# A graph attention layer on one core: the node stage moved beside the first chunk of edges

## The chip, the cores and the metric

The kernel runs on one core of one Trainium2 chip, in one launch. The core has TensorE (PE) for matmuls, VectorE (DVE), ScalarE (ACT), GpSimd (POOL) and SyncE (SP); SP, ACT and POOL also issue transfers, which share 16 DMA engines. Each engine takes its instructions in the order in which the compiled program lists them. The metric is the time on the device in microseconds (us), lower is better. Before the change the median of 18 runs is 6028.96 us (6012.63 to 6041.9).

## The reference

A layer norm with relu, one graph attention layer over 12500 nodes of 128 features and 412500 directed edges, and a residual. Cut to what is computed:

```python
h_in = jnp.maximum(_layernorm(x), 0.0)
h = h_in @ Wn + bn;  q = h_in @ Wq + bq;  k = h_in @ Wk + bk;  v = h_in @ Wv + bv
eh = edge_attr_64 @ We + be
attn_in = jnp.concatenate([q[src], k[dst], eh], axis=-1)
hmid = leaky_relu(attn_in @ A1 + b1, 0.2)
scores = leaky_relu(hmid @ A2 + b2, 0.2)
w = softmax(scores.mean(axis=-1), axis=0)          # over all edges
out = segment_sum(w[:, None] * v[dst], src, num_segments=12500)
y = h + out
return x + gamma * (y - y.mean(-1)) / sqrt(y.var(-1) + 1e-5) + beta
```

The edges are sorted by `dst`. The softmax runs over all edges at once, and the sum goes by `src`, which is in no order.

## The kernel before, in words

Nodes are padded to 12544, that is 98 blocks of 128, and edges to 403 groups of 1024 (eight tiles of 128). As the edges lie by `dst`, a group touches some 31 consecutive nodes. The groups are cut into four chunks of 86, 121, 121 and 75.

**Preparation.** `indices()` works out, on DVE, each edge's block and place by `src` and its offset in its group's window of 42 nodes (`WIN`) by `dst`; the window's first node stands in `base_i`. An edge outside its group's window would be left for `other_edges()`. The weights are folded (`w_all`, `w_ea`).

**Nodes.** `nodes()` handles 20 tiles of five blocks: load x (L552, SP), normalise (L361 to L372, DVE, with the square L365 and the root L370 on ACT), transposes (L561, PE), relu into `hT` (L563, ACT), one matmul with all weights (L569), and q, k, v each split into three bf16 parts by copies (L579, L587 on ACT, L581 on DVE) and matmuls that subtract what was copied (L582, L584). ACT then issues the writes of `hn_tab`, `q_tab` and `kv_tab` (L588 to L590). A tile holds, in each of the 128 partitions p, five neighbouring nodes of the 98 that begin at 98 p, so a transfer has one run of five rows per partition, and every window of `kv_tab` needs nodes of nearly all tiles.

**Finding slots.** `ready(c)` counts chunk c's edges by block (`count`, L391 to L408), plans (`plan`), and finds every edge a slot in the chunk's table (`place_slots`: per five edge tiles two matmuls L478, a reduction L522, a comparison L471, a small L526; every 40 edge tiles `settle`).

**First stage.** For each group `load` fetches edge features (L667), the window of k and v (L671) and the offsets (L673); `select` makes the selection matrix (L681, DVE). Per pair of edge tiles (four per group, called banks here) PE sums edge and node parts into `row_ps` (L705, L708). `evict` copies places into column 0 of four rows of a ring of 16 rows (L688, ACT, for every second bank) and the bank into two rows (L691, ACT), and POOL scatters each row tile into the chunk's table (L645, an indirect DMA): eight scatters per group. The ring holds two groups, so L688 of a group waits until the scatters of the group two before it have landed. The loads run two groups ahead, with three buffers.

**Second stage.** `second_stage()` reads the sorted table of the chunk before by blocks of 128 `src` nodes (L728) with the block's queries (L731), and works out scores, weights and sums.

**What sets the order.** The count, the plan and the first steps of slot finding, the 20 node tiles and the 98 clears of the first table's ends (`clear_ends`, L168, 257 KB each, SP) are interleaved first; there SP keeps the program's order and a scheduler, by its own costs, orders the other engines. `kv_tab` is read at addresses known only at run time, so a window waits for every `kv_tab` write that stands before it in the program. Then comes one pass per chunk: the first stage of chunk c, the second stage of chunk c-1, `ready(c+1)` and the clears of table c+1, interleaved; in these passes PE, DVE, ACT and SP keep the program's order (`manual_schedule`, L1026). The pass of the first chunk holds its first stage, the rest of its slots and `ready(1)`; the second stage begins after it.

Of the kernel before, what the change touches and what calls it, by code (L numbers as in the profile page):

```python
# [22 lines left out]
P = 128  # L23
# [30 lines left out]
NGRP = 5  # L54
CHUNKS = (0.213, 0.3, 0.3, 0.187)
# [3 lines left out]
def _ceil(a, b):  # L59
    return -(-a // b)  # L60
# [44 lines left out]
def kernel(ctx: ExitStack, tc: tile.TileContext, n_edges, x, src, dst, ea, w_nv, w_qt, w_kt,  # L105
# [43 lines left out]
    q_tab = dram.tile([NTN, P, 3 * D], BF, name="q_tab")  # L149
# [90 lines left out]

    early = ExitStack()
    weights = early.enter_context(tc.tile_pool(name="weights", bufs=1))
    w_all = weights.tile([P, 4, D], FP, name="w_all")
    bias_all = weights.tile([P, 4, D], FP, name="bias_all")
    early.enter_context(tc.manual_schedule(engines={ET.SP}))
# [6 lines left out]

    with tc.tile_pool(name="prep", bufs=1) as prep, tc.tile_pool(name="prep_ps", bufs=1, space=PSUM) as pps:
        nc.sync.dma_start(out=w_all[:, 0, :], in_=w_nv[0])
        nc.sync.dma_start(out=w_all[:, 3, :], in_=w_nv[1])
        a1_sb = prep.tile([P, 3, D], FP, name="a1_sb")
        nc.sync.dma_start(out=a1_sb, in_=a1.rearrange("(s p) d -> p s d", p=P))
        wt = prep.tile([P, 3, D], FP, name="wt")
        for i, w in enumerate((w_qt, w_kt, w_et)):
            nc.sync.dma_start(out=wt[:, i, :], in_=w)  # L260
        col = prep.tile([P, 3], FP, name="col")
        nc.sync.dma_start(out=col, in_=cols)
        fold = pps.tile([P, 4, D], FP, name="fold")
        for i in range(3):
            nc.tensor.matmul(fold[:, i, :], lhsT=wt[:, i, :], rhs=a1_sb[:, i, :], start=True, stop=True)
        nc.vector.tensor_copy(w_all[:, 1:3, :], fold[:, 0:2, :])
        for b in range(2):
            nc.vector.tensor_copy(w_ea[b * DE:(b + 1) * DE, b, :], fold[b * DE:(b + 1) * DE, 2, :])
        colb = prep.tile([P, 3, P], FP, name="colb")
        for i in range(3):  # L270
            nc.vector.tensor_copy(colb[:, i, :], col[:, i:i + 1].to_broadcast([P, P]))
        bias_ps = pps.tile([P, D], FP, name="bias_ps")
        for i in range(3):
            nc.tensor.matmul(bias_ps, lhsT=colb[:, i, :], rhs=a1_sb[:, i, :], start=(i == 0), stop=(i == 2))
        nc.vector.tensor_copy(bias_all[:, 0, :], row_bc[:, 0, :])
        nc.vector.tensor_add(bias_all[:, 1, :], bias_ps, row_bc[:, 2, :])
        nc.vector.memset(bias_all[:, 2, :], 0.0)
        nc.vector.tensor_copy(bias_all[:, 3, :], row_bc[:, 1, :])

# [11 lines left out]
    np_ = early.enter_context(tc.tile_pool(name="nodes", bufs=2))  # L291
    tps = early.enter_context(tc.tile_pool(name="t_ps", bufs=2, space=PSUM))
    mps = early.enter_context(tc.tile_pool(name="m_ps", bufs=4, space=PSUM))

    def indices():
# [14 lines left out]
        if t_end < NT:  # L310
# [7 lines left out]
        nc.vector.tensor_scalar(head, offset[0:1, :].rearrange("p (g k) -> p g k", k=SUPER)[:, :, 0],  # L318
                                float(NP - WIN), None, op0=ALU.min)
# [36 lines left out]
    indices()  # L356

    def normalise(pool, y, n):
# [12 lines left out]
        nc.vector.reciprocal(r[:, :n], r[:, :n])  # L371
        nc.vector.tensor_mul(y, y, r[:, :n].unsqueeze(2).to_broadcast([P, n, D]))  # L372

    x_v = x.rearrange("(p t) d -> p t d", p=P)
    hn_v = hn_tab.rearrange("(p t) d -> p t d", p=P)
    kv_v = kv_tab.rearrange("(p t) d -> p t d", p=P)
    q_v = q_tab.rearrange("t p d -> p t d")


    start_of = {}  # L380

    def count(c):

# [710 lines left out]
```

## Time and profile before

| | |
|---|---|
| median of 18 runs | 6028.96 us |
| the profiled execution | 6031.0 us, span 6029.3 us |
| first scatter | 372.75 us |
| first scatter of the second chunk (the 689th) | 1308.08 us |
| first load of a table block for the second stage (L728) | 1309.58 us |
| PE, DVE, ACT, POOL busy over the span | 83%, 74%, 35%, 56% |
| mean granted PE clock | 0.92 |

The span runs from the first to the last instruction of the profiled execution. Rows of a stage give the busy time of each engine between two moments, with the number of instructions, and then the PE clock that was granted (1 is full speed), the mean busy share of the 16 DMA engines and the GB/s that they moved. A row of waits names the engine and line that waited, what it waited for, the time in total, how often, and the longest. In the timeline a row has the start, the duration, the engine (with a q: the issue of a transfer), the line, the operation with the tile written and the tiles read, and in brackets the idle time before it and what ended it.

### The profile page before, as it was taken

The page shows a single profiled execution, that of the slowest core. Times are in us where ns is not written, and L with a number is a line of the kernel's source. Part 1 is how long each engine was busy: PE and PEld are TensorE (multiplying, and loading weights), DVE is VectorE, ACT ScalarE, POOL GpSimd, SP SyncE. Part 2 cuts the span into 40 slices and gives each one's busy share as a digit, 9 for nine tenths or more (in the row PEclk, how much of TensorE's full clock was granted, in tenths as well). Part 3 has the DMA queues.
Part 4 walks back from the last instruction along what each step waited for, and adds up shares of the span by engine and source line. Part 5 has one row for each costly group of instructions (what it writes and reads, how often), then busy time and mean ns, then how long its engine had stood idle before and what let it go on. Part 6 is the DMA issues. An engine that isn't in the chain of part 4 may idle for free. (4 is left out here: it accounts for less than half of the span.)

```text
span 6029.3 us, 99478 instructions
## 1 busy us (share of the span) xinstructions
PE 4997.8 (83%) x31822; PEld 3443.8 (57%) x32180; DVE 4461.5 (74%) x14096; ACT 2120.5 (35%) x5090; POOL 3391.9 (56%) x3236
## 2 busy tenths in 40 slices
PE   5766766669998899889999999989999999888880
PEld 3333433336666666556666666657777777666650
DVE  8765766658777777767777777767777777777779
ACT  2432222224333343334444434434444444333321
POOL 0047777777777777767777777756565555000000
PEclk8887678779999999989999999989999999999995
DMA  6755555568888888878898888877888887444433
GB/s 190 217 189 166 166 167 174 170 189 251 265 252 257 260 256 256 263 223 266 271 280 284 283 269 276 269 232 266 259 264 265 263 266 245 154 152 152 153 126 128
DMA packets 607563, 1362.14 MB, mean 226 GB/s; under 512 B 120100, under 2 KB 336860, under 8 KB 569016
## 3 DMA queue, kind: packets, MB, share of 16 engines
q1 hardware_dynamic: 423572, 880.87, 49.5%
q0 software_dynamic: 154704, 424.26, 19.5%
q10 hardware_dynamic: 28756, 50.57, 2.6%
q8 instruction: 255, 4.18, 0.3%
q14 instruction: 276, 2.26, 0.1%
HBM read 782.14 MB, written 573.14 MB: 225 GB/s over the span
## 5 line engine op out<-in xcount | busy, mean ns | idle before, releaser
L645 POOL DMA_INDIRECT tab<-row,slots x3223 | 3390.2, 1052 | 1726.6 <-issue 731.2
L705 PE MATMUL row_ps<-w_ea,ea_t 128*128 128x256 f32 x3224 | 1093.3, 424 | 292.4 <-ACT row L691 253.7
L691 ACT ACTIVATE row<-row_ps 128x512 f32<-128x512 f32 x1612 | 933.1, 588 | 477.5 <-PE row_ps L708 452.4
L859 PE MATMUL o_ps<-rows_of,w 128*128 128x128 f32 x7252 | 1081.8, 291 | 13.4 <-DVE w L850 12.4
L850 DVE TENSOR_SCALAR w<-iota_f,rows_of,score 128x128 f32<-128x128 f32 x3626 | 1021.8, 353 | 6.6
L776 DVE TENSOR_TENSOR rows_of<-h_ps,low 128x512 f32<-128x512 f32 (+1 forms) x980 | 634.8, 648 | 482.4 <-ACT low L775 480.6
L705 PEld LDWEIGHTS row_ps<-w_ea,ea_t 128*128 128x128 f32 x3224 | 601.2, 208 | 639.7 <-ACT row L691 424.5
L859 PEld LDWEIGHTS o_ps<-rows_of,w 128*128 128x128 f32 x7252 | 915.2, 195 | 43.9 <-DVE w L850 25.9
L775 ACT ACTIVATE low<-h_ps 128x512 f32<-128x512 f32 (+1 forms) x980 | 552.2, 563 | 870.5 <-PE h_ps L767 862.2
L767 PE MATMUL h_ps<-sel_q,qw 128*128 128x512 bf16 (+1 forms) x2582 | 720.7, 365 | 50.1 <-DVE sel_q L755 29.2
L708 PE MATMUL row_ps<-kv,sel 126*128 126x256 bf16 x3224 | 662.8, 289 | 12.0 <-DVE sel L681 12.0
L522 DVE TENSOR_REDUCE num<-run 128x5 f32<-128x500 f32 x646 | 433.4, 671 | 297.2 <-PE run L478 296.7
L764 PE MATMUL h_ps<-ident,rows_of 128*128 128x128 f32 x3626 | 572.9, 278 | 0.0
L784 PE MATMUL s_ps<-rows_of,a_sb 128*32 128x512 f32 (+1 forms) x1960 | 462.0, 586 | 65.1 <-DVE most_of L831 45.5
L688 ACT ACTIVATE row<-place 128x4 f32<-128x4 bf16 x806 | 162.9, 202 | 997.2 <-DMA tab<-row,slots 979.7
L801 PEld LDWEIGHTS s_ps<-heads,z 96*128 96x128 f32 (+1 forms) x3136 | 389.8, 193 | 206.6 <-DVE z L795 188.8
L708 PEld LDWEIGHTS <-sel 126*128 126x128 bf16 x3224 | 337.6, 105 | 291.0 <-issue 56.7
L764 PEld LDWEIGHTS h_ps<-ident,rows_of 128*128 128x128 f32 x3626 | 435.0, 143 | 109.1 <-issue 83.0
L801 PE MATMUL s_ps<-heads,z 96*128 96x3 f32 (+1 forms) x3136 | 412.6, 252 | 89.1 <-DVE z L795 88.7
L791 ACT ACTIVATE z<-s_ps,b_col 64x512 f32<-64x512 f32 (+1 forms) x392 | 266.9, 681 | 525.9 <-PE s_ps L784 525.3
L471 DVE TENSOR_TENSOR one<-bins_b,block 128x500 f16<-128x500 bf16 x646 | 431.3, 668 | 0.3 <-PE run L478 0.3
L755 DVE TENSOR_SCALAR sel_q<-pls,part 128x1408 bf16<-128x1408 uint8 (+2 forms) x392 | 331.6, 846 | 117.9 <-DMA pls<-pl_d 109.3
(178 smaller groups left out, 4808.5 us busy)
## 6 DMA issues: line engine op xcount, KB each, us to landing
rows_of<-tab SPq DMA_DIRECT2D x196, 1413.5 KB
ea_t<-in_ea SPq DMA_DIRECT2D x403, 256.0 KB
tab<-blank SPq DMA_DIRECT2D x392, 257.0 KB
rows_of<-tab SPq DMA_DIRECT2D x98, 1028.0 KB
rows_of<-tab SPq DMA_DIRECT2D x98, 899.5 KB
tab<-row,slots POOLq DMA_INDIRECT x3223
offs<-off_d SPq DMA_DIRECT2D x403, 126.0 KB
qw<-q_tab SPq DMA_DIRECT2D x392, 96.0 KB
```

The lines of the kernel that those rows point to most:

```text
L645: i = nc.gpsimd.indirect_dma_start(out=tabs[c][:, :], out_offset=bass.IndirectOffsetOnAxis(ap=slots[c][t // (8 * STR)][:m, t % (8 * STR):t ...
L691: nc.scalar.activation(row[:, :, 1:ROW], bank, AF.Copy)
L705: nc.tensor.matmul(bank[:, :, 0:D], lhsT=ea_g[:, ts(k, P)], rhs=w_ea, start=True, stop=False, skip_group_check=True)
L708: nc.tensor.matmul(bank[:, b, :], lhsT=sel[:, ts(b * halves + k, P)], rhs=kv, start=False, stop=True, skip_group_check=True)
L764: nc.tensor.matmul(h_ps[:, ts(j, P)], lhsT=rows_of[i][:, q * QUAD + j, 1:D + 1], rhs=ident, is_transpose=True, start=j == 0, stop=False, s ...
L767: nc.tensor.matmul(h_ps[:, 0:m * P], lhsT=qws[i][:, ts(k, D)], rhs=plss[i][:, q * QUAD * P:(q * QUAD + m) * P], start=False, stop=k == 2, ...
L775: nc.scalar.activation(low, h_ps, AF.Copy, scale=SLOPE)
L776: nc.vector.tensor_max(rows_of[i][:, q * QUAD:q * QUAD + m, 1:D + 1], h_ps.rearrange("p (j e) -> p j e", j=m), low.rearrange("p (j e) -> p ...
L784: nc.tensor.matmul(state["s_ps"][32 * q:32 * (q + 1), 0:m * P], lhsT=a2_sb, rhs=rows_of[i][:, q * QUAD:q * QUAD + m, 1:D + 1], start=True, ...
L801: nc.tensor.matmul(state["s_ps"][:, 0:nq * QUAD].rearrange("p (q j) -> p j q", j=QUAD)[:, j, :], lhsT=state["z"][:32 * nq, ts(j, P)], rhs= ...
L850: nc.vector.tensor_scalar(w, iota_f, rows_of[i][:, t, 0:1], state["score", i][:, t:t + 1], op0=ALU.is_equal, op1=ALU.mult)
L859: nc.tensor.matmul(state["o_ps"][:, 0:D], lhsT=w, rhs=rows_of[i][:, t, D + 1:ROW], start=t == 0, stop=t == ct - 1)
```

## The change

A node tile now holds 640 consecutive nodes (views `(t p) d` in place of `(p t) d`), so that the first windows need the first tiles alone. `q_tab` goes by node; the second stage reads a block's queries as rows that lie 98 nodes apart. Three node tiles are worked out ahead of the first chunk (`FIRST + 1`). The rest come inside its pass: before the window load of group g, `nodes_for(g)` puts as many tiles as are needed to have 1280 + 210 g nodes done (`FIRST`, `AHEAD`), one tile in about three groups, up to group 52. A window's base is held to what is done by then, `min(dst, NP - WIN, 1238 + 210 g)`. Writes of `kv_tab` are declared free of the windows read before. The node pools live until the end of the first chunk's pass, with one `t_ps` and three `m_ps` buffers instead of two and four, and the second stage's pools are opened after it. The first chunk's pass is no longer written out by hand on PE, DVE and ACT: only SP keeps the program's order, and the scheduler orders the others. The folding of the weights stands behind `indices()`.

```diff
@@ constants
+FIRST = 2
+AHEAD = 210
@@ tables
-    q_tab = dram.tile([NTN, P, 3 * D], BF, name="q_tab")
+    q_tab = dram.tile([NP, 3 * D], BF, name="q_tab")
@@ indices()
-        nc.vector.tensor_scalar(head, offset[0:1, :].rearrange("p (g k) -> p g k", k=SUPER)[:, :, 0],
-                                float(NP - WIN), None, op0=ALU.min)
+        bound_i = xp.tile([1, NG], I32, name="bound_i")
+        nc.gpsimd.iota(bound_i, pattern=[[AHEAD, NG]], base=FIRST * NGRP * P - WIN, channel_multiplier=0)
+        bound = xp.tile([1, NG], FP, name="bound")
+        nc.vector.tensor_scalar(bound, bound_i, float(NP - WIN), None, op0=ALU.min)
+        nc.vector.tensor_tensor(head, offset[0:1, :].rearrange("p (g k) -> p g k", k=SUPER)[:, :, 0], bound, op=ALU.min)
@@ views
-    hn_v = hn_tab.rearrange("(p t) d -> p t d", p=P)
-    kv_v = kv_tab.rearrange("(p t) d -> p t d", p=P)
-    q_v = q_tab.rearrange("t p d -> p t d")
+    x_c, hn_c, kv_c, q_c = (v.rearrange("(t p) d -> p t d", p=P) for v in (x, hn_tab, kv_tab, q_tab))
+    win_loads = []
@@ nodes()
-            nc.sync.dma_start(out=xt[:, :n, :], in_=x_v[:, t0:t0 + n, :])
+            nc.sync.dma_start(out=xt[:, :n, :], in_=x_c[:, t0:t0 + n, :])
...
-            nc.scalar.dma_start(out=hn_v[:, t0:t0 + n, :], in_=hn[:, :n, :])
-            nc.scalar.dma_start(out=q_v[:, t0:t0 + n, :], in_=parts[:, :n].rearrange("p t s d -> p t (s d)"))
-            nc.scalar.dma_start(out=kv_v[:, t0:t0 + n, :], in_=parts2[:, :n].rearrange("p t s d -> p t (s d)"))
+            i = nc.scalar.dma_start(out=kv_c[:, t0:t0 + n, :], in_=parts2[:, :n].rearrange("p t s d -> p t (s d)"))
+            for other in win_loads:
+                tc.declare_no_dep(i.ins, other, reason="windows before lie in nodes that were done by then")
+            nc.scalar.dma_start(out=hn_c[:, t0:t0 + n, :], in_=hn[:, :n, :])
+            nc.scalar.dma_start(out=q_c[:, t0:t0 + n, :], in_=parts[:, :n].rearrange("p t s d -> p t (s d)"))
@@ before the chunks
-    first_ready = ready(0)
-    interleave((some_steps(first_ready, ready_enough()), ready_enough()), (nodes(), _ceil(NTN, NGRP)),
-               (clear_ends(0), NTN))
+    np_ = setup.enter_context(tc.tile_pool(name="nodes", bufs=2))
+    tps = setup.enter_context(tc.tile_pool(name="t_ps", bufs=1, space=PSUM))
+    mps = setup.enter_context(tc.tile_pool(name="m_ps", bufs=3, space=PSUM))
+    node_loads = nodes()
+    done = [0]
+
+    def nodes_for(g):
+        while done[0] * NGRP * P < min(NP, FIRST * NGRP * P + AHEAD * g):
+            next(node_loads)
+            done[0] += 1
+
+    first_ready = ready(0)
+    def first_nodes():
+        for i in range(FIRST + 1):
+            nodes_for(_ceil(i * NGRP * P - FIRST * NGRP * P + 1, AHEAD))
+            yield
+
+    interleave((some_steps(first_ready, ready_enough()), ready_enough()), (first_nodes(), FIRST + 1),
+               (clear_ends(0), NTN))
@@ first_stage(), load(g)
-            nc.sync.dma_start(out=kv, in_=win_v[ds(state["bases"][i % 8] * 3, 3 * WIN), :])
+            nodes_for(g)
+            i = nc.sync.dma_start(out=kv, in_=win_v[ds(state["bases"][i % 8] * 3, 3 * WIN), :])
+            win_loads.append(i.ins)
@@ second_stage(), load(i)
-            nc.sync.dma_start(out=qws[i], in_=q_tab[b])
+            nc.sync.dma_start(out=qws[i], in_=q_tab.rearrange("(p t) d -> t p d", p=P)[b])
@@ the passes
-        with tc.manual_schedule(engines={ET.PE, ET.DVE, ET.Activation, ET.SP}):
+        if c == 0:
             interleave(*jobs)
+            for _ in node_loads:
+                pass
+            setup.close()
...
+        else:
+            with tc.manual_schedule(engines={ET.PE, ET.DVE, ET.Activation, ET.SP}):
+                interleave(*jobs)
```

What order the compiled programs have on ACT in the first chunk can be read without running them. Here p9a and p9b are the copies of places (L688) for the first and second two banks of group 9, r9 the four evictions (L691) of group 9, sq and sqrt L365 and L370, hT L563, KV the issue of a tile's `kv_tab` write (L590), and the node tile's other copies stand between hT and KV:

```
before  ... p7a r7(0,1) p7b r7(2,3) p8a r8(0,1) p8b r8(2,3) p9a r9(0,1) p9b r9(2,3) ...
after   ... KV r7(0-3) p9a r8(0,1) p9b r8(2,3) r9(0,1) p10a r9(2,3) p10b sq p11a sqrt p11b hT hT KV r10(0-3) ...
```

## Prediction

> **What bounds the kernel now.** I read the busy table and the 40 slices first, then the busy time by stage, then who waited for whom inside the first chunk, then the timeline where the node stage ends.
>
> ```profile
> span 6029.3 us, 99478 instructions
> POOL 0047777777777777767777777756565555000000
> 0.00:373.00 373.00, 231.13 (x1458) 125.12 (x1459) 273.93 (x875) 146.04 (x475) 1.95 (x14) 0.84 0.70 203
> 373.00:1309.00 936.00, 613.11 (x3091) 343.78 (x3090) 604.41 (x1685) 212.90 (x523) 711.03 (x689) 0.78 0.52 168
> 1309.00:6030.00 4721.00, 4153.56 (x27274) 2974.93 (x27632) 3583.11 (x11538) 1761.60 (x4092) 2678.89 (x2535) 0.95 0.76 239
> ```
>
> The stage rows give busy us of PE, PE's weight loads, DVE, ACT and POOL, then the granted clock, the DMA share and GB/s. POOL, which issues the row scatters, does nothing for 373 us while the nodes are worked out. Then the first chunk's 688 scatters run from 372.75 to 1308.08, 1.36 us each, with POOL busy 76% and PE and DVE at 65%: this stage is set by the rate of scatters, and everything after it moves with its end.
>
> ```profile
> ACT row L688 <- DMA tab<-row,slots: 577.8, 145, 8.8
> POOL tab L645 <- DMA kv<-kv_tab: 370.4, 1, 370.4
> POOL tab L645 <- issue: 163.9, 538, 0.3
> 342.91 0.59 ACT L563 ACTIVATE hT<-tp 128x512 f32<-128x512 f32 x1
> 349.63 0.34 ACTq L590 DMA_DIRECT2D kv_tab<-parts  x1
> 361.39 0.34 ACTq L590 DMA_DIRECT2D kv_tab<-parts  x1
> 366.41 0.41 SPq L671 DMA_DIRECT2D kv<-kv_tab  x1
> 370.41 0.75 DVE L681 TENSOR_SCALAR sel<-offs,third 126x1024 bf16<-126x1024 uint8 x1 [9.84 <-DMA offs<-off_d]
> 371.86 0.60 ACT L691 ACTIVATE row<-row_ps 128x512 f32<-128x512 f32 x1 [10.33 <-PE row_ps L708]
> 372.75 1.36 POOL L645 DMA_INDIRECT tab<-row,slots  x1 [370.38 <-DMA kv<-kv_tab]
> ```
>
> Two things are to be seen. First, within the first chunk ACT stands still for 577.8 us of 936 at L688, the copy of the places into the row ring, because the scatters that read the ring (16 rows, two groups) have not landed. Today that is harmless: nothing else is queued on ACT in this stage. Matching L688 with the scatter it waits for, the wait ends 3.4 us (median; 2.6 to 5.4 from the tenth to the ninetieth of 144 waits) after that scatter's start. Second, from a node tile's last table write to the first scatter that depends on it take 372.75 - 361.39 = 11.4 us: write 5.0, window and offsets 4.0, selection, matmul and eviction 2.3.
>
> **The change part by part.**
>
> *Start of the scatters.* Only three of the 20 node tiles stand ahead of the first window. DVE is busy 273.9 us before the first scatter; a node tile costs it 9.7 us (its rows L361 to L372, L573, L574, L581 sum to 194 us for 20), so 17 tiles take 165 away and leave 109, which at today's 73% share is 149 us. The third tile's x load stands on SP behind 82 clears of 257 KB, 21.6 MB; with the indices and two tiles some 31 MB, that is 107 us at 290 GB/s (203 divided by its share 0.70) or 152 at 203, from 15 us on: at 122 to 167, say 145. Behind it come its load and normalisation (about 13), its matmuls (11, below) and the 11.4 above. First scatter at 180, with overheads 185 (165 to 215): 188 us earlier (158 to 208).
>
> *Node tiles inside the first chunk.* The other 17 tiles come one per three groups, before the loads of groups 4, 7, ... 52. Their engine time fits: per three groups at today's pace (33 us) DVE has some 31 us of work and PE about as much, if everything overlapped. It does not, because of the order in which the compiled program puts ACT's instructions. From the cycle of groups 7 to 9 (row = L691, place = L688): rows of 7, 8 and 9, place 10, sq, place 11 first half, sqrt, place 11 second half, hT (L563), the tile's copies, the kv_tab write (L590), rows of 10. Place 11 second half overwrites ring rows that group 9's last four scatters read. So hT waits on ACT until every scatter issued so far has landed; and group 10's window, one of this tile's nodes, can only be loaded after its kv_tab write. The same stands in all 17 cycles. POOL runs dry once per tile. What is queued behind the waiting place copy is ACT's whole node tile, behind that DVE's and PE's parts of it, SP's window load (with the clears and loads of later groups behind it), and at last POOL.
>
> One such drain: landing 3.4 (2.6 to 5.4), place copy 0.2, hT to the kv_tab write 11 (6.7 in the lines above, where a tile had ACT nearly to itself; 11.2, 12.5 and 14.3 at 265.80, 280.35 and 295.29, with counting work between; the changed order puts about four steps of slot finding between, so I take the lower of these), write to first scatter 11.4 (10 to 14: the write is 960 KB against 576, but the queue ahead is emptier), less the 1.36 of an ordinary step. 24.6 us (18 to 32), times 17: 418 (306 to 544).
>
> The other waits sit under this. The x load waits on SP for the ea buffer of the group three earlier, free some 8 us into the next cycle; load and normalisation then have the 31 us of 24 scatters. DVE's steps of slot finding (0.68 + 0.67 + 0.17 us, and 2.1 us from one to the next at 371 to 379) stall with the node tile, but about ten of 15 per cycle fit in the drain. If that cover were too small, each further step would add 2.1 us a cycle.
>
> *Order of the rest of the chunk.* From group 65 on the place copies of the next two groups stand ahead of the next group's rows, so ACT waits for a landing every second group: 11 times (3.4 + 0.2 + 0.6 + 0.3 - 1.36 = 3.1), 34 us (0, if POOL is late anyway, to 60).
>
> *Edits at nothing.* The x, hn and kv_tab transfers go from 2560 and 7680 bytes a run to 512 and 1536, the bytes are the same and the first chunk uses 0.52 of the DMA engines; if that failed, the write's 5.0 us grow, which the 14 above holds. The queries of the second stage are still 768 bytes a run, loaded many steps ahead; today 392 loads of 96 KB (0 to +20 us if their spread rows are slower). The window bound (1238 + 210 per group) lies above the data's 31 nodes per group, so no edge is left over. Weights and prep move behind the indices: a few us, in the 185. Later chunks keep their order.
>
> The Trainium skill (DMA: Bandwidth & Descriptors, Anatomy of one DMA) puts a transfer's fixed cost at about 2.0 us. By that a drain would lose 1.4 on the landing, about 0.8 on the 960 KB write (2.0 plus 2.2 at its 436 GB/s) and 1.8 on the window and offsets, and the 17 would cost 350, the sum 6227; the trace's 3.4, 5.0 and 4.0 decide.
>
> *Sum,* against the profiled execution's 6031.0 us (its span is 6029.3; the median of 18 runs is 6029.0, so 2 less): -188 + 418 + 34 = +264, 6295; on the median 6293, and I say 6290.
>
> **The rivals.**
>
> Faster, by hidden nodes: ACT finds the ring's scatters landed when it reaches the place copies, so hT runs beside the scatters. For it: at today's start of the chunk (L688 in the first four groups) there is no wait, and PE and DVE have a third of their time free. Against: 145 of the later copies waited, and in the new order ACT evicts three groups in a burst, well ahead of POOL. Price: 6031 - 188 = 5843 in full; it decides once a drain costs under (188 - 34) / 17 = 9.1 us, less than the 11.4 of the table path alone.
>
> Half drains: hT waits only for the group before the last, so some ten of the 25 us lie under the last eight scatters (8 times 1.36 = 11). 17 times 14 = 238, sum +84: 6115. For it: some tiles have their first hT ahead of the last place copy (three of 17). Against: their copies stand behind it all the same.
>
> Longer drains: DVE's slot finding, held up behind the waiting node tile, is not caught up, five steps of 2.1 us more a cycle: 17 times 35 = 595, sum +441, 6470. For it: DVE's order is fixed too, and PE's granted clock, 0.78 now, may fall when PE idles (0.59 in the last 180 us, where PE is busy 16%). Against: ten steps fit in the drain.
>
> Not what it says: the first scatter comes hardly earlier, at 300, since SP's clears hold the third x load. Then +264 + 115 = 6410. Against: 290 GB/s is enough for them.
>
> **How the numbers follow.** Full drains 68%, half drains 12%, longer drains or a late start 12%, hidden nodes 6%, no change to be measured 2%. The likeliest alone: 6160 (start 208 earlier, drains 19 us each, tail 15) to 6420 (start 170 earlier, drains 31, tail 30). The range takes in half drains and most of the longer: 6095 to 6440. About 0.2% is what can be told from no change: faster 6%, same 2%, slower 92%.
>
> **What would show it.** After: first scatter near 185 us; POOL in the first chunk with 17 gaps of some 25 us, each ended by an eviction that waited for PE, PE for the selection, that for the offsets; ACT's place copies ahead of each hT waiting for the scatters; the first load of rows_of near 1570; later stages as long as before. I am wrong if POOL's gaps are under 10 us, if they end at the x load or at DVE's slot finding, or if the stages after the first chunk change by more than 20 us.

## The result, and the profile after

The changed kernel takes 6384.25 us (median of 8 runs, 6370.55 to 6391.17) against 6031.07 for the kernel before beside it: a ratio of 1.0585, with a 95% interval of 1.0574 to 1.0596. It is slower, by 353 us. The profiled execution took 6372.4 us.

From its page, the span and POOL's busy tenths over the 40 slices:

```profile
span 6370.7 us, 99183 instructions
...
POOL 0334433476577777776777777775555555100000
```

And the busy time by stage (us, then PE, weight loads, DVE, ACT and POOL busy, the granted clock, the share of the DMA engines, GB/s): before the first scatter, the stretch with node tiles, the rest of the first chunk, everything after it.

```profile
0.00:225.00 225.00, 89.31 (x893) 48.99 (x894) 147.60 (x464) 26.57 (x80) 2.12 (x14) 0.74 0.86 178
225.00:1239.00 1014.00, 567.30 (x2755) 293.68 (x2756) 514.57 (x1518) 256.50 (x712) 418.56 (x417) 0.70 0.40 128
1239.00:1648.00 409.00, 227.68 (x772) 118.93 (x772) 199.99 (x503) 87.30 (x203) 275.80 (x273) 0.72 0.50 157
1648.00:6371.00 4723.00, 4154.86 (x27404) 2969.93 (x27761) 3603.03 (x11615) 1762.50 (x4097) 2672.86 (x2535) 0.95 0.76 239
```

The last row says where the time is not: everything from the second chunk on takes 4723 us, before 4721. The first scatter comes at 225.07 instead of 372.75 (147.7 earlier), the 689th at 1647.78 instead of 1308.08. The first chunk went from 935 to 1423 us, and in its first 1014 us no engine is busy for more than 56%: DVE 51%, PE 56%, POOL 41%. It waits. In that stretch POOL has 17 gaps, one per node tile, from 19.7 to 34.2 us, 488 in all, 28.7 on the mean. (A gap is counted here from the start of one scatter to the start of the next; the idle time in brackets is some 1 us shorter.) One of them in the timeline, all engines in order of time:

```profile
354.61 0.46 SPq L527 DMA_DIRECT2D xt<-in_x  x1
...
382.27 0.96 POOL L662 DMA_INDIRECT tab<-row,slots  x1 [0.31 <-issue]
384.94 0.21 ACT L707 ACTIVATE row<-place 128x4 f32<-128x4 bf16 x1 [4.65 <-DMA tab<-row,slots]
385.05 0.58 ACT L538 ACTIVATE hT<-tp 128x512 f32<-128x512 f32 x1
402.05 0.38 ACTq L563 DMA_DIRECT2D kv_tab<-parts  x1
406.36 0.36 SPq L689 DMA_DIRECT2D kv<-kv_tab  x1
412.51 1.09 ACT L710 ACTIVATE row<-row_ps 128x512 f32<-128x512 f32 x2 [10.31 <-PE row_ps L727]
413.38 0.96 POOL L662 DMA_INDIRECT tab<-row,slots  x1 [30.15 <-ACT row L710]
```

This is the chain of the prediction, link by link: the last scatter (382.27), the place copy that waits for its landing (384.94), hT directly behind it, the tile's work on ACT up to the table write (402.05), the window load that waits for that write (406.36), the eviction, the next scatter. Over the 17 gaps the medians are 2.8 us from the last scatter to hT, 15.9 from hT to the write, 10.7 from the write to the scatter. Who waited for whom in the first chunk (us in total, times, longest) shows ACT's wait for landings much as before (577.8 us then), and POOL's wait for an eviction, 20.5 us before:

```profile
ACT row L707 <- DMA tab<-row,slots: 606.6, 165, 10.5
POOL tab L662 <- ACT row L710: 525.6, 82, 33.2
```

So the chain stood as foretold, in 12 of the 17 cycles with a place copy directly ahead of hT; in the other five the tile's root stands there and hT follows its transposes. Whether each link *causes* the loss is another question, and there the experiments did not follow the prediction.

### The profile page after: what moved, and what is told of

Its sections match the earlier page's. It is cut to its first block, busy times and chain, and to the rows that moved or that the text cites. A ratio compares the mean times of both kernels' runs of the same rounds, so it can differ in the third digit from the quotient of the medians.

```text
span 6370.7 us, 99183 instructions
## 1 busy us (share of the span) xinstructions
PE 5039.1 (79%) x31822; PEld 3431.5 (54%) x32180; DVE 4465.2 (70%) x14097; ACT 2132.9 (33%) x5090; POOL 3369.3 (53%) x3237
## 5 line engine op out<-in xcount | busy, mean ns | idle before, releaser
L878 PEld LDWEIGHTS o_ps<-rows_of,w 128*128 128x128 f32 x7252 | 909.7, 194 | 45.7 <-DVE w L869 27.8
L700 DVE TENSOR_SCALAR sel<-offs,third 126x1024 bf16<-126x1024 uint8 x403 | 305.1, 757 | 194.1 <-DMA offs<-off_d 188.3
```

What stands on the lines that cost most here:

```text
L878: nc.tensor.matmul(state["o_ps"][:, 0:D], lhsT=w, rhs=rows_of[i][:, t, D + 1:ROW], start=t == 0, stop=t == ct - 1)
```

## Experiments

They ran on three chips, which differ in the later stages (see the last section), so each ratio is to the kernel before on the same chip, and the first chunk is read by itself. "Chunk" is the time from the first scatter to the 689th; "gaps" is the mean of the 17 longest gaps in it, without the one at the chunk's border. They lie at the 17 node tiles, but for the two kernels with freed windows, where some of the tiles' gaps are too short to count among them.

| kernel | chip | ratio to before (95%) | first scatter | chunk | gaps |
|---|---|---|---|---|---|
| changed | (first comparison) | 1.0585 (1.0574 to 1.0596) | 225 | 1423 | 28.7 |
| changed, once more | C | 1.0566 (1.0538 to 1.0594) | 231 | 1518 | 31.6 |
| program order | A | 1.0428 (1.0387 to 1.0470) | 225 | 1461 | 28.3 |
| program order, ACT and SP only | A | 1.0534 (1.0502 to 1.0566) | 224 | 1555 | 34.1 |
| tile three groups ahead | A | 1.0448 (1.0429 to 1.0466) | 227 | 1458 | 28.7 |
| all nodes first | A | 1.0179 (1.0162 to 1.0195) | 396 | 1126 | none |
| tile ahead, windows freed | B | 1.0239 (1.0213 to 1.0265) | 219 | 1222 | 12.9 |
| ring of 32 rows | B | 1.0621 (1.0590 to 1.0651) | 252 | 1425 | 29.1 |
| first tiles early | B | 1.0616 (1.0588 to 1.0645) | 241 | 1440 | 29.4 |
| fine tiles | B | 0.9877 (0.9846 to 0.9907) | 264 | 971 | none |
| no place copies | C | 1.0512 (1.0490 to 1.0535) | 229 | 1492 | 31.4 |
| no place copies, tile ahead, windows freed | C | 1.0131 (1.0107 to 1.0154) | 218 | 1247 | 13.0 |
| fine tiles, lead grows | C | 0.9924 (0.9905 to 0.9943) | 245 | 1100 | none |

The kernel before takes 6600 us on chip A, 6068 on B, 6611 on C. The changed kernel itself, run again on chip C:

> The changed kernel as it is, beside the three kernels below on one chip, since the chips differ in the stages after the first chunk (4723 to 5232 us). Expected: 1.056 to 1.063 times the kernel before, 17 gaps with a mean of 28 to 31 us, first scatter at 220 to 255.

Its ratio is the same within the intervals; its gaps, 31.6 us, lie just above the 28 to 31 expected.

### The order on ACT

The theory on record was that the scheduler's place copies, put ahead of hT, make ACT wait for all scatters. The first test gives the first chunk back its written order.

```diff
-            interleave(*jobs)
+            with tc.manual_schedule(engines={ET.PE, ET.DVE, ET.Activation, ET.SP}):
+                interleave(*jobs)
```

> The changed kernel with one edit: the first chunk's PE, DVE, ACT and SP instructions run in the order in which the program emits them, as the later chunks' do. On ACT a node tile's squares, root, hT, copies and kv_tab write then stand together, behind the rows of the group just before and ahead of the next group's place copies. Theory (the scheduler's place copies, put ahead of hT, make ACT wait for all scatters, so POOL is drained once per tile): hT no longer waits for a landing; the tile's 17 us on ACT and the 11 us from its write to the next scatter run beside the last group's 8 to 16 scatters (11 to 22 us). The 17 gaps of POOL shrink from 28.7 us to 8 to 16, so 220 to 350 us less than the changed kernel's 6384: 6035 to 6165. Rival (the cause is not the order on ACT but the chain tile, write, window, whichever way it is ordered): the gaps stay at 25 us or more and the time at 6340 or more.

> As the program-order kernel, but only ACT's and SP's instructions of the first chunk keep the program's order; PE and DVE stay with the scheduler. Theory (ACT's order alone is what drains POOL): the same as with all four engines, 6035 to 6165 us, gaps of 8 to 16 us. Rival (DVE's slot finding or PE's order holds the node tile): gaps stay near 28 us and the time near 6384, and only the kernel with all four engines in program order is faster.

The gaps did not shrink: 28.3 and 34.1 us. (By their ratios, times 6031, the two would take 6289 and 6353: both outside the theory's range, and the first below its rival's 6340 as well.) One gap of the kernel with all four engines in program order, all engines in order of time:

```profile
417.25 0.43 SPq L527 DMA_DIRECT2D xt<-in_x  x1
419.78 0.96 POOL L662 DMA_INDIRECT tab<-row,slots  x1 [0.30 <-issue]
...
427.36 0.60 ACT L538 ACTIVATE hT<-tp 128x512 f32<-128x512 f32 x1 [2.29 <-PE tp L536]
...
445.54 0.39 ACTq L563 DMA_DIRECT2D kv_tab<-parts  x1
...
448.05 1.06 ACT L710 ACTIVATE row<-row_ps 128x512 f32<-128x512 f32 x2
448.90 0.96 POOL L662 DMA_INDIRECT tab<-row,slots  x1 [28.16 <-ACT row L710]
```

No landing is waited for ahead of hT, and no window behind the write (write to scatter 3.4 us instead of 10.7; the windows of these rows had been loaded). In their place the tile comes in one piece: x is loaded only 2.5 us before the last scatter, hT starts 7.6 after it, the tile takes 18.2 us on ACT (20.6 in the median of 17), and the rows of the next group stand behind it on PE, DVE and ACT alike. With ACT's order alone the square waits up to 29.3 us for DVE. The theory's sentence "the tile's 17 us run beside the last scatters" was wrong: POOL had at most a few scatters left when the tile began. The lower ratio with all four engines (1.0428; the changed kernel has 1.0566 on chip C and was not run on chip A) is not found in the 17 gaps; one part is the chunk's border, 2.3 us instead of 19.3, and the rest was not traced.

### The windows

> The changed kernel with one edit: each load step takes the group's window first and then the node tile that the group three later needs, so no window waits for a tile that was only just written; the scheduler still orders the first chunk. Theory (two parts in a row make a drain: landing, place copy and 17 us of ACT's tile ahead of the next rows, and 11 us from the tile's write to the next scatter): only the second part goes, since ACT still waits for the landings ahead of hT. The gaps go from 28.7 to 18 to 22 us, 17 times 7 to 11 us less: 6200 to 6265. Rival 1 (the window chain alone is the cause): no gaps above 5 us, 5900 to 5960. Rival 2 (it hides nothing, since the ring's waits set all): 6384 within 30.

```diff
             kv = p2.tile([3 * WIN, 2 * D], BF, name="kv")
-            nodes_for(g)
             i = nc.sync.dma_start(out=kv, in_=win_v[ds(state["bases"][i % 8] * 3, 3 * WIN), :])
             win_loads.append(i.ins)
+            nodes_for(g + 3)
```

The gaps are 28.7 us, the changed kernel's own: none of the theory's 7 to 11 us a gap is to be seen. (By its ratio it would take 6301, which is in neither the theory's range nor the rival's; the changed kernel was not run on this chip, and the gaps don't hold the difference.) By the gaps the second rival comes nearest, but not for its reason. A window waits for every write of `kv_tab` that stands before it in the program, whether it reads from it or not. With the tile put earlier, the tile just written is a later one, and the window waits for it all the same. One gap:

```profile
365.30 0.96 POOL L662 DMA_INDIRECT tab<-row,slots  x1 [0.30 <-issue]
...
382.18 0.38 ACTq L563 DMA_DIRECT2D kv_tab<-parts  x1
386.45 0.40 SPq L688 DMA_DIRECT2D kv<-kv_tab  x1
...
392.78 0.96 POOL L662 DMA_INDIRECT tab<-row,slots  x1 [26.52 <-ACT row L710]
```

So the next kernel also says which writes a window does not need (`start` is a tile's first node):

```diff
+            node_writes.append((t0 * P, i.ins))
...
             win_loads.append(i.ins)
+            for start, other in node_writes:
+                if start >= FIRST * NGRP * P + AHEAD * g:
+                    tc.declare_no_dep(i.ins, other, reason="the window lies in nodes before this tile")
```

> As the kernel with tiles three groups ahead of their windows, with one more edit: a window's load no longer counts as depending on the kv_tab writes of tiles that it doesn't need (there every window waited for every table write emitted before it, so SP and POOL still stood until the tile just written was in the table). The rows of the next group can now run beside the tile. Theory (the drain is held by the windows' wait for the newest tile; once that is gone only the place copies that stand ahead of hT and of the kv_tab write wait for landings): the 17 gaps of 28.7 us fall to one or two waits of 4 to 10 us per tile, 10 to 18 us a tile, 180 to 320 us off the changed kernel; on a chip where that takes 6384, 6065 to 6205. Rival (the place copies ahead of hT alone drain POOL, the windows don't matter): gaps stay at 20 us or more, less than 150 us off.

This took the gaps to 12.9 us and the chunk to 1222 us. Two kernels on the same chip whose windows still wait as in the changed one, with the ring of 32 rows and with the early first tiles, have 29.1 and 29.4 us and chunks of 1425 and 1440. The changed kernel's ratio would give 6423 on this chip, so it is some 215 us faster, inside the range. One gap:

```profile
429.62 0.58 ACT L539 ACTIVATE hT<-tp 128x512 f32<-128x512 f32 x1
...
447.12 0.96 POOL L664 DMA_INDIRECT tab<-row,slots  x1 [0.30 <-issue]
450.97 0.38 ACTq L564 DMA_DIRECT2D kv_tab<-parts  x1
455.23 0.40 SPq L690 DMA_DIRECT2D kv<-kv_tab  x1
...
462.60 0.96 POOL L664 DMA_INDIRECT tab<-row,slots  x1 [14.52 <-ACT row L715]
```

hT now runs 24.8 us (median) before the last scatter ahead of the group that needs the tile: rows are made beside the tile. What is left is the table path, write to window to eviction, 13.3 us in the median. It is left because the tile is worked on for three groups, so its write comes (median) 1.9 us before that last scatter, when the window that needs it is next. The place copies still wait here (512.8 us in total from 220 to 1300), so the part that the prediction named first is there, and the gaps are short all the same.

"Needs" is by the bound of 1280 + 210 g nodes, which the edit above uses, and not by the data. At some 31 nodes a group the windows of all 86 groups of the first chunk end near node 2670, in the fifth tile, so only two of the 17 tiles inside the chunk are ever read by them; the others are wanted by the later chunks and by the second stage. A tighter bound for the windows alone, at the same pace of the tiles, would free nearly all of them; no run tried it.

### The landing ahead of hT

> The changed kernel with one edit: the first chunk's row ring has 32 rows instead of 16 (four groups), so the place copies ahead of hT wait for scatters that were issued two groups earlier; the windows' wait for the newest tile stays. Theory 1 (ACT's wait for the landing of the last scatters ahead of hT starts the drain): hT runs beside the last 8 to 16 scatters, so 10 to 20 us of the tile's 17 and the table path's 11 are hidden; the gaps fall from 28.7 to 9 to 18 us, 180 to 330 us off the changed kernel (6055 to 6205 where that takes 6384). Theory 2 (the tile's x load, behind the ea buffers on SP, or its chain through DVE sets when hT runs): gaps within 3 us of 28.7, less than 60 us off.

```diff
+    rring0 = setup.enter_context(tc.tile_pool(name="pr0", bufs=1)).tile([P, 2 * RROWS, ROW], FP, name="row")
...
-            at = ((g - g0) * halves + k) * 2 % RROWS
-            row = rring[:, at:at + 2, :]
+            ring, depth = (rring0, 2 * RROWS) if c == 0 else (rring, RROWS)
+            at = ((g - g0) * halves + k) * 2 % depth
+            row = ring[:, at:at + 2, :]
```

The gaps are 29.1 us, which looks like theory 2, but the test did not take away what it meant to:

```profile
411.00 0.96 POOL L663 DMA_INDIRECT tab<-row,slots  x1 [0.30 <-issue]
413.77 0.21 ACT L709 ACTIVATE row<-place 128x4 f32<-128x4 bf16 x1 [4.76 <-DMA tab<-row,slots]
413.88 0.58 ACT L538 ACTIVATE hT<-tp 128x512 f32<-128x512 f32 x1
```

The copy ahead of hT still waits for the last scatter (2.77 us after its start). In the compiled order the scheduler had used the deeper ring to put the place copies two groups further ahead, to the rows of the group just before. So this run does not decide between the two. The next one leaves the copies out:

```diff
+    nc.gpsimd.memset(rring, 0.0)
...
-            if k % 2 == 0:
+            if k % 2 == 0 and c > 0:
                 nc.scalar.activation(rring[:, at:at + 4, 0:1].rearrange("p (k b) r -> p k (b r)", b=2),
```

> The changed kernel without the place copies of the first chunk: the ring's first column is set to zero once and stays so (the places of the first chunk's rows are left out, so later sums are not the reference's). The windows still wait for the tile just written. With no copy ahead of it, hT stands behind the last eviction of the group before, which waits only for scatters two groups old. Theory (the place copies ahead of each hT make ACT wait for the last landing, and that is where the drain begins): hT runs 12 to 20 us earlier, beside the last scatters; the gaps fall from 28.7 to 11 to 18 us, 180 to 300 us off the changed kernel. Rival (hT waits for its x load, for DVE or for PE anyway; the place copies only happen to stand there): gaps of 24 us or more, less than 80 us off.

The rival's numbers: gaps of 31.4 us beside 31.6 of the changed kernel on the same chip, 29 us off the time. One gap, ACT and POOL:

```profile
383.95 0.60 ACT L711 ACTIVATE row<-row_ps 128x512 f32<-128x512 f32 x1 [4.34 <-remote]
390.28 0.60 ACT L711 ACTIVATE row<-row_ps 128x512 f32<-128x512 f32 x1 [5.73 <-remote]
396.58 0.60 ACT L711 ACTIVATE row<-row_ps 128x512 f32<-128x512 f32 x1 [5.70 <-remote]
398.71 1.46 POOL L663 DMA_INDIRECT tab<-row,slots  x1 [0.30 <-issue]
...
405.66 0.60 ACT L538 ACTIVATE hT<-tp 128x512 f32<-128x512 f32 x1 [3.00 <-PE tp L536]
421.13 0.38 ACTq L563 DMA_DIRECT2D kv_tab<-parts  x1
432.95 0.96 POOL L663 DMA_INDIRECT tab<-row,slots  x1 [32.78 <-ACT row L711]
```

With no copy in its way, hT comes not earlier but 7.2 us after the last scatter (median of 17; 5.9 in the changed kernel on this chip): now the last evictions wait, with the tile's square, root and transposes behind them. They do not wait for the ring: the scatters 16 places back, which it would ask for, had started 13 to 21 us before the three waits shown ended. They wait for PE. The trace's record of semaphores has a count by PE within 0.1 us before each of the three ends (383.88, 390.20, 396.51), though the view names no releaser. Why PE is so late stays open.

These late evictions belong to the chip as well. On chip C the changed kernel has them too (waits from the first scatter to the 689th), and on chip A the program-order kernel; the same view of the first comparison and of the kernels on chip B has no such row:

```profile
ACT row L710 <- remote: 145.6, 30, 8.4
```

So on chip C the copies are not what holds hT: already in the changed kernel hT follows the end of its transposes at once in 13 of 17 cycles. In the first comparison it starts 2.5 us after that end (median; at most 7.4), behind a place copy in 12 cycles, and a kernel without copies was not run on such a chip. How much an earlier hT is worth can be seen in four cycles of this run, where it came 9 to 15 us before the last scatter: their gaps are 17.0 to 26.7 us, the other thirteen 33.8 on the mean.

Removing the copies from the kernel with freed windows gives the fourth corner:

> Both taken away: tiles three groups ahead of windows that wait only for the tiles they need, and no place copies in the first chunk (left out, as in the kernel before this one). The node tiles' work itself and the scheduler's order stay. Theory (the landing wait ahead of hT and the windows' wait for the newest tile are the two causes, and there is no third): gaps of 0 to 6 us, the tail's gaps gone too, 400 to 490 us off the changed kernel, 20 to 120 us under the kernel before. Rival (a third cause, DVE or PE short of time beside the tiles): gaps of 8 us or more, less than 350 us off.

Gaps of 13.0 us, 284 us off the changed kernel on this chip and 81 above the kernel before: the rival's result. Read as a square, tiles ahead with freed windows are worth 16 us a gap with the copies (29.1 to 12.9, chip B) and 18 without them (31.4 to 13.0, chip C), and leaving out the copies takes nothing off the gaps in either row (31.6 and 31.4 on chip C; 12.9 on chip B against 13.0 on chip C). The place copy is on the chain in the profile, and as a cause it is not shown. The third cause that this rival asked for is mostly no shortage of engine time: it is the table path above (13.4 us here), since a tile three groups ahead is finished just when the bound asks for it. The evictions that wait for PE are there too, and their share of these gaps was not measured.

### All nodes first

```diff
-FIRST = 2
+FIRST = 20
```

> The changed kernel with one number changed: all 20 node tiles stand ahead of the first chunk (as in the kernel before), still tiles of consecutive nodes, and the scheduler still orders the first chunk. It separates the tiles inside the chunk from the other edits. Theory: the first scatter is back near 373 us, the 17 gaps are gone, and what stays is the scheduler's order of place copies, a landing wait of 3 to 5 us nearly every second group (30 to 40 of them) and an empty stretch of some 18 us at the chunk's border: 6031 + 50 to 130, that is 6080 to 6160. Rival (the other edits and the scheduler's order cost nothing, all of the loss is the tiles inside the chunk): 6025 to 6050.

1.0179, some 120 us above the kernel before on its chip: the theory's range, though the first scatter came at 396. No node tile is left in the chunk; what remains are 25 gaps of 4 to 10 us, two long ones (18.9 and 31.1) and the border's 19.5, 212 us together. In the first long one SP stands for 19.79 us at the flag writes of slot finding, and the loads of the next groups are queued behind them:

```profile
786.51 19.79 SPq L459 DMA_DIRECT2D flag_d<-rank  x3
```

So with no node tile in the first chunk a third of the loss is still there, and the tiles inside the chunk make the rest. That the scheduler's order makes this third, and not another of the edits, is argued from such gaps; no run has all nodes first in program order.

### The start

> The changed kernel with one number changed: before the first chunk the three node tiles are spread over the first quarter of the clears, so that their x loads stand on SP behind about 4, 12 and 20 clears in place of 16, 43 and 82. Nothing in the first chunk changes: the 17 gaps and the time from the first scatter to the last of the chunk are the changed kernel's own. Theory A (the third x load behind SP's clears, issued at 171 us, sets the start): the first scatter comes near 185 us instead of 225, 35 to 45 us off the whole. Theory B (the transfers themselves, 178 GB/s at a share of 0.85, set it, whichever comes first on SP): first scatter at 210 or later, at most 15 us off.

```diff
-    interleave((some_steps(first_ready, ready_enough()), ready_enough()), (first_nodes(), FIRST + 1),
+    interleave((some_steps(first_ready, ready_enough()), ready_enough()), (first_nodes(), 12),
```

Theory B. Some of SP's issues in this kernel (start, and the time that the group of issues took):

```profile
72.20 0.39 SPq L527 DMA_DIRECT2D xt<-in_x  x1
...
137.50 76.19 SPq L170 DMA_DIRECT2D tab<-blank  x50
...
232.14 0.40 SPq L689 DMA_DIRECT2D kv<-kv_tab  x1
```

All three x loads are out by 72 us, 99 earlier than the third was, and still the first scatter comes at 241, 11 us before that of the 32-row ring on the same chip (252), which starts as the changed kernel does. The count's result, which the next clears stand behind on SP, is out at 136 instead of 110, and then 50 clears take 1.5 us each; the first window is behind them. The third x load was the last link of the chain in the changed kernel, but the clears stand right beside it.

### A version that beats both kernels

From all this follows a kernel that does what the change set out to do: the first chunk in program order, tiles in 19 small steps between the banks, x loaded a tile ahead, the tile ready well before its first window, and windows that wait only for what they read. `nodes()` yields after the load, each step of the normalisation, each hT and each step of the splits; the windows' part is the edit shown above.

```diff
-AHEAD = 210
+AHEAD = 140
...
+            if t0 + NGRP < NTN:
+                ahead = load_x(t0 + NGRP)
+            yield
...
+    def nodes_beside(g):
+        while node_step[0] < NSTEP * (FIRST * NGRP * P + AHEAD * g) / (NGRP * P) and tiles_done[0] * NGRP < NTN:
+            next(node_loads)
+            node_step[0] += 1
...
                 if k == 1 and g + 1 < g0 + n:
                     select(g + 1)
+                if c == 0:
+                    nodes_beside(g + k / halves + 7)
                 yield
```

> A version without the three parts of the drain: the first chunk in program order on PE, DVE, ACT and SP; each node tile cut into 19 small steps, about one step emitted behind each bank of two rows, x loaded one tile ahead; the tile finished some five groups ahead of the first window that reads it, and windows that don't count later tiles as their sources; one tile per 4.6 groups in place of 3 (140 nodes a group); the first three tiles early among the clears. Theory (every part of the drain was order, not work: DVE and PE had a third of their time free): no gap of POOL above 8 us, the chunk's 688 scatters in 935 to 1010 us, first scatter at 185 to 225: 150 to 300 us off the time of the changed kernel's chunk end (1648), the whole 5850 to 5960 on a chip where the kernel before takes 6031, a ratio of 0.970 to 0.988. Rival (the node tiles' work doesn't fit beside the rows, one of DVE, ACT or PE becomes the bound): the scatters' pace falls from 1.36 to 1.7 us or more, chunk of 1150 us or more, ratio 1.01 or more.

Ratio 0.9877: faster than the kernel before by 1.2%, than the changed kernel by about 7%, by the two ratios. Its busy time in the first chunk and after it:

```profile
264.00:1235.00 971.00, 671.85 (x3654) 387.90 (x3653) 743.65 (x2114) 328.58 (x910) 716.71 (x688) 0.86 0.65 197
1235.00:5983.00 4748.00, 4184.67 (x27632) 2983.13 (x27632) 3584.03 (x11542) 1762.02 (x4092) 2679.04 (x2535) 0.95 0.76 238
```

The chunk takes 971 us with all 17 tiles in it (935 without them in the kernel before, on the first chip), DVE at 77%, PE at 69%, POOL at 74%, and POOL's longest gap is 7.6 us. So the work fits. Several edits came in at once here, and which of them gave how much was not measured. The first scatter was later than expected, 264; in the program 12 steps of the fourth tile stand ahead of the first rows. The last run lets the lead grow:

```diff
-                    nodes_beside(g + k / halves + 7)
+                    nodes_beside(g + k / halves + min(7, 4.5 + 0.8 * g))
```

> The version with the node tiles in 19 small steps, with one edit: the steps' lead over the windows starts at 4.5 groups and grows to 7 over the first three groups, so that not 12 steps of the fourth tile stand ahead of the first rows (there the first scatter came at 264 us, 20 us after the first selection). Expected: first scatter 12 to 22 us earlier for the same start of the windows, the chunk's length unchanged (971, within 20), ratio 0.983 to 0.988 of the kernel before. Rival (the steps only move into the chunk and stretch it by as much): ratio unchanged at 0.988 or more.

The first scatter came 19 us earlier, as expected, but on another chip, where the chunk took 1100 us instead of 971 and the ratio was 0.9924 (0.9905 to 0.9943), on the rival's side. Whether the ramp helps can't be told from runs on two chips; both versions beat the kernel before.

## Why the prediction was right, and where it was not

The forecast, 6290 us and slower at 92%, with a range to 6440, held: 6384. The likeliest case came true, by 94 us too cheap.

*Start of the scatters.* 225 where 185 was given, and 165 to 215 as its bounds. The term that failed is the third x load at 145: it was issued at 170.86, since the 33 clears before it took 1.7 us each. The rate of 290 GB/s, worked out from a share of 0.70, was not reached: 186 GB/s at a share of 1.10 from 120 to 180 us. Where the load stands on SP was not what held the start: 99 us earlier brought 11 us (chip B, one profile each), with the clears next on the chain. From the load to hT took 18.5 us instead of 13, hT to the write 25.0 instead of 11 (the same term as in the drain below); the write to the scatter 10.7 instead of 11.4. The rival of a late start at 300 named this and overstated it.

*Node tiles.* 17 gaps, one for each tile, each ended by an eviction: right. 27.4 us each beyond an ordinary step instead of 24.6, 465 in all instead of 418. The terms: landing and place copy 2.8 (given 3.6), hT to write 15.9 (given 11, "the lower of these"; the mis-sized one), write to scatter 10.7 (given 11.4). The step of the sum that was mis-sized has a reason: the prediction's cases for it were misread. Each pairs a tile's hT with the write of the tile before it. Behind the hT at 342.91 in the trace of before come one more tile's hT and two writes besides the one at 349.63 that was taken for its own:

```profile
352.12 0.53 ACT L563 ACTIVATE hT<-tp 128x384 f32<-128x384 f32 x1
357.11 0.34 ACTq L590 DMA_DIRECT2D kv_tab<-parts  x1
```

The last tile (three blocks, hT at 352.12) is written at 361.39, so the tile of 342.91 is written at 357.11: 14.2 us where 6.7 was read. The other three cases are 27 to 29 us, with counting work between, where 11.2 to 14.3 were read. With 14.2 the same sum gives 27.8 a drain and 473 in all.

*Its reason.* "So hT waits on ACT until every scatter issued so far has landed" describes the trace, and the sum built on it was near. As a cause it is not shown: without the place copies the gaps are 31.4 us beside 31.6, on a chip where PE holds the evictions as well. Nor does group 10's window read "one of this tile's nodes": at 31 nodes a group it lies near node 310, in the first tile. It waits for the write because the write stands before it in the program. Shown as a cause is this wait for the tile just written: with the tile three groups ahead and the windows freed of it the gaps fall to 12.9 us (29.1 and 29.4 beside it on chip B) and to 13.0 (31.4 beside it on chip C); the tile three groups ahead alone leaves 28.7. The tile's position (in one piece, and late) is the likely rest; the version with fine steps removes it together with other things. "Half drains" (14 us a gap) is not what the changed kernel shows, though hT came before the last scatter in four of the 17 cycles.

*Order of the rest.* 34 us were given for 11 landings; six gaps of 4.4 to 5.7 us (22 beyond the steps) and, not foreseen, 19.3 us at the chunk's border, ended by PE's slot finding for the next chunk.

*Edits at nothing.* Nothing to be seen after the chunk: 4723 us against 4721. *Longer drains*: no; slot finding runs inside the gaps. *Hidden nodes*: the changed kernel does not have them; 9.1 us a drain was named as the point from which that side decides, and the fine version, with no drain, is on it.

*The rule weighed.* The Trainium skill (DMA: Bandwidth & Descriptors, Anatomy of one DMA) has about 2.0 us as the fixed cost of a transfer issued from GpSimd. Here a scatter, which is one, has landed 2.7 us after its start in the lines above, where the wait for it ends; the 960 KB write, issued from ACT, takes 4.3 us (median) until the window behind it is issued, against the 5.0 of the smaller one in the trace of before and the 4.2 that the page's figures would make, an estimate. By the page the sum was 6227, further off than 6290.

In sum: -148 for the start instead of -188, +465 instead of +418, +22 and +18 instead of +34, and -18 because the other 664 steps of the chunk took 885 us and not 664 times 1.36: +339, which is the chunk's end at 1648 instead of 1308. (The 353 at the top compare medians; the profiled executions differ by 341.)

## What to carry to other kernels

A wait that stands in the chain of a profile is a link, not yet a cause: before it is named as one, take away what makes it wait and see whether the next wait takes its place, as the evictions' wait for PE did here for the place copies, and do it on the chip that showed the chain. In these programs a read at an address known at run time waits for every write to its tensor that comes before it in the program; putting the producer earlier left the gaps at 28.7 us until the reader said which writes it needs. When two events of a stream are paired to read a duration, count both to the end of the stream: here the pairing was one tile off, and 14.2 us were read as 6.7. And a tile that is cut as fine as the loop and finished well before its first reader hid beside it here, while in one piece it did not.

## What the runs showed of the hardware

The same program differs between chips by up to 10%, and only in part by the clock. In the row of the changed kernel's later stages on chip C, beside the last of the four rows at the top:

```profile
1748.00:6970.00 5222.00, 4382.62 (x27763) 3071.68 (x27761) 3623.75 (x11616) 1750.04 (x4097) 2656.96 (x2535) 0.92 0.69 216
```

5222 us against 4723, at a granted clock of 0.92 against 0.95; the share of the DMA engines times the stage's length is the same (3603 and 3589), so the same transfers took the same engine time and more stood between them. In the first chunk one part is the evictions' wait for PE (above); in this stage it was not looked into. On chips A and B this stage is 5194 to 5232 and 4748 to 4774 us, so the ratio of two kernels that differ in the first chunk alone depends on the chip, and the chunk should be read by itself.

The clears at the start, 257 KB written to device memory each, drain at 1.5 to 1.7 us apiece, 155 to 173 GB/s, and the share of the DMA engines then reads 0.9 to 1.1: GB/s over share, taken from the same stage of the kernel before (290), was no measure of what they could move.
